# Layer 1's silu from the exponential's table with a VectorE reciprocal, and the last chunk's DMAs begun from two queues

## The chip, the cores and the metric

The kernel runs on one core of one Trainium2 chip. The metric is the device time of one execution in microseconds (us). The kernel before took 1212.17 us (median of three runs, 1210.58 to 1214.08). A core has a matrix engine (PE, which writes only to PSUM), VectorE (DVE), ScalarE (ACT), GpSimd (POOL) and a queue engine (SP); each works through its own list of instructions in order and waits on semaphores for the others. DMAs are begun by an instruction on SP, ACT or POOL.

## The reference

Two transformer layers over x of shape 2 x 1024 x 256, as 16 tiles of 128 rows. Each layer normalises x, and adds an attention and a feed-forward part of the same normalised input:

```python
xn = layernorm(x); x = x + attn0(xn) + ffn0(xn)
xn = layernorm(x); x = x + attn1(xn) + ffn1(xn)
```

The change is in layer 1. Its feed-forward part, with ternary weights `wq_gu` (2048 x 256) and `wq_p` (256 x 1024), is

```python
gate, up = split(xn @ wq_gu.T)          # 1024 columns each
h = silu(gate) * up                     # silu(g) = g / (1 + exp(-g))
out = rms_norm(h) @ wq_p.T
```

Its attention is odd: in every token, the 16 heads of 16 values attend to each other (a 16 x 16 softmax per token), with a rotary embedding before and an output projection `wo` after.

## The kernel before, in words

Layer 0 runs until about 797 us of the profiled execution and is not touched. Layer 1 (`layer1`, L390) treats x in four chunks of 512 tokens, in the order 0, 1, 3, 2. The order of the work is written down ahead of time: `at(delay, f)` puts a piece of work in a heap with a due time, and L673 to L675 take the pieces out in order of due time; PE keeps exactly that order (`manual_schedule` for PE), while the other engines' lists are put in order by a scheduler.

Per chunk there are four *blocks* b of attention and eight *units* hc of the feed-forward part, two units to a block. The pieces, with their lines:

- `project` (L429): the q, k, v projections of 128 tokens. PE writes `pqk` and `pv`; VectorE makes two products with the rotary tables (L442), POOL adds them (L448), ScalarE copies `pv` out (L456). `turn` (L459) transposes on PE (`pt`, L464), ScalarE copies (L465), and SP sends the result through DRAM into the slots (`qkv`, L467 and L469).
- `scores` (L478): PE writes `sq` (L484) to a buffer of four banks that exists once (`ps_s`, bufs=1); VectorE takes the maximum (L492), which goes through DRAM into a row of the slots (L494, L497).
- `turn_v`, `shifted` (L503, L513): PE transposes v (`vt`, L508), then writes the shifted scores `sk` (L519) to the same one `ps_s` buffer, and ScalarE takes the exponential `p` (L527). The next block's `sq` needs the buffer back, and so waits for `p`.
- `weighted`, `normalise`, `turn_back` (L530, L545, L559): `acc` (L534), copied to `o` (L542); transposed to `ot` (L548); VectorE's reciprocal `z` of the 16 sums (L550) and the product `on` (L552); `ob` (L564), copied to `rows` (L565). After the fourth block of a chunk the rows go through DRAM with four DMAs (`orows`, L574) and come back with two (`turned`, L578), then `attended` (L582) multiplies by `wo` (`ao`, L585) and adds to x (L586).
- `ffn_unit` (L598): eight matmuls, four for the gate and four for the up half, into two PSUM banks `ps[0]`, `ps[1]` of the pool `ps_gu`. The pool has two banks in all, so a unit's gate matmuls wait until the last reader of the previous unit's `ps[0]` is done, and its up matmuls until the last reader of `ps[1]` is. ScalarE takes silu of `ps[0]` (L616), VectorE multiplies by `ps[1]` (L617), POOL squares and sums (L621, L623).
- `ffn_scale`, `ffn_out` (L625, L636): the sum over the hidden columns (`pss`, L629), its inverse root (a Sqrt on ScalarE, L145), and the second matmul `f1o` (L640), added to x by VectorE (L648).

`done` (L591) sends a tile of x to the output once both parts are in (L594). All small PE results of the pieces above share the PSUM pool `ps_m` of two banks.

In a middle block PE's order is: `acc`, `pt`, first unit, `ot`, `vt`, second unit, `ob`, `sk`, `pqk`, `pv`, then `sq` of the next block. In the last chunk there is no `project` left, so `sq` follows `sk` directly. In the block that holds the previous chunk's `f1o`, the matmuls of `f1o` stand between the units.

Silu, Exp and Sqrt are in different function tables of ScalarE here: between them stands an `ACT_TABLE_LOAD`.

Of the kernel before, what the change touches and what calls it, by code (L numbers as in the profile page):

```python
# [10 lines left out]
F32 = mybir.dt.float32  # L11
# [3 lines left out]
AF = mybir.ActivationFunctionType  # L15
ALU = mybir.AluOpType
# [3 lines left out]
P = 128  # L20
# [28 lines left out]
def two_layers(ctx: ExitStack, tc: tile.TileContext, a: dict, out: bass.AP):  # L49
    nc = tc.nc  # L50
# [6 lines left out]
    xs = [cp.tile([P, D], F32, tag=f"x{i}", name=f"x{i}") for i in range(NT)]  # L57
# [16 lines left out]
    for name, op, fill, sign in (  # L74
# [5 lines left out]
        for e in range(2):  # L80
            for t in range(2):
                part = m[HALF * e : HALF * e + HALF, t, :]
                nc.gpsimd.affine_select(
                    out=part,
                    in_=part,
# [304 lines left out]
    def layer1(w, wgu, wp, cs, sc):  # L390
# [7 lines left out]
        scale = 1.0 / HD**0.5  # L398
        with ExitStack() as es:
            pool = es.enter_context(tc.tile_pool(name="l1", bufs=2))  # L400
# [6 lines left out]
            chunks = (0, 1, 3, 2)  # L407
# [4 lines left out]
            for n in range(2):  # L412
                q, k, v = (pool.tile([P, NH, P], F32, tag=f"{x}{n}", name=f"{x}s{n}", bufs=1) for x in "qkv")
                nc.gpsimd.memset(v, 1.0)
                for s in range(4):
                    nc.sync.dma_start(
                        out=k[S * s + HD : S * s + HD + 9], in_=a["same"][0, :, None, :].to_broadcast([9, NH, P])
                    )
                    nc.sync.dma_start(
                        out=q[S * s + HD : S * s + HD + 8], in_=a["same"][1, 0:8, None, :].to_broadcast([8, NH, P])  # L420
# [124 lines left out]
            def normalise(c, b, o):  # L545
                ps = ps_m.tile([P, 4, 4, S], F32, tag="m", name=f"ot{c}{b}")
                for r in range(4):
                    nc.tensor.transpose(ps[:, r].rearrange("p s d -> p (s d)"), o[:, r, :], ident)  # L548
                z = pool.tile([P, 4, 4, 1], F32, tag="z1", name=f"z1_{c}{b}")
                nc.vector.reciprocal(z, ps[:, :, :, HD : HD + 1])  # L550
                on = won[b % 2]
                nc.vector.tensor_tensor(  # L552
                    on[:, :, :, 0:HD], ps[:, :, :, 0:HD], z.to_broadcast([P, 4, 4, HD]), ALU.mult
                )
                at(0.9, lambda: turn_back(c, b, on))
# [3 lines left out]
            def turn_back(c, b, on):  # L559
                if b == 0:  # L560
                    rows[c] = pool.tile([P, NH, P], F32, tag="rows", name=f"rows{c}", bufs=1)
                ps = ps_m.tile([P, 4, P], F32, tag="m", name=f"ob{c}{b}")
                for r in range(4):
                    nc.tensor.transpose(ps[:, r], on[:, r].rearrange("p s d -> p (s d)"), ident)  # L564
                nc.scalar.copy(  # L565
                    rows[c].rearrange("p h (t r) -> p (h t) r", r=16)[:, :, 4 * b : 4 * b + 4],
                    ps.rearrange("p r n -> p n r"),
                )
                if b < 3:
                    return  # L570
                scr = dram.tile([D, 4, P], F32, tag="orows", name=f"orows{c}")
                turned = pool.tile([P, 2, 4, P], F32, tag="turned", name=f"turned{c}", bufs=1)
                for s in range(4):
                    nc.sync.dma_start(  # L574
                        out=scr[:, s].rearrange("(h d) t -> d h t", d=HD), in_=rows[c][S * s : S * s + HD]
                    )
                for k in range(2):
                    nc.sync.dma_start(out=turned[:, k], in_=scr[k * P : (k + 1) * P])  # L578
                for s in range(4):
                    at(2.2 + 0.4 * s, lambda s=s: attended(c, s, turned))  # L580

            def attended(c, s, turned):  # L582
                ps = ps_m.tile([P, D], F32, tag="m", name=f"ao{c}{s}")
                for k in range(2):
                    nc.tensor.matmul(ps, turned[:, k, s], wo[:, k, :], start=(k == 0), stop=(k == 1))  # L585
                nc.vector.tensor_add(xs[4 * c + s], xs[4 * c + s], ps)  # L586
                done(4 * c + s)
# [3 lines left out]
            def done(t):  # L591
                parts_done[t] += 1
                if parts_done[t] == 2:
                    nc.sync.dma_start(out=out[t // 8, (t % 8) * P : (t % 8 + 1) * P, :], in_=xs[t])  # L594

            hidden = {}

            def ffn_unit(n, hc):  # L598
                if hc == 0:
                    hidden[n] = [], pool.tile([P, 512], F32, tag="ss", name=f"ss{n}")  # L600
                hs, ss = hidden[n]
                if hc % 2 == 0:
                    hs.append(pool.tile([P, 2, 512], F32, tag="h", name=f"h{n}_{hc}", bufs=6))
                h = hs[-1][:, hc % 2, :]
                nm = f"{n}_{hc}"
                ps = [ps_gu.tile([P, 512], F32, tag="gu", name=f"f1gu{nm}_{g}") for g in range(2)]
                for g in range(2):
                    for k in range(2):
                        nc.tensor.matmul(  # L609
                            ps[g],  # L610
                            wgu[:, k, g * HID + hc * P : g * HID + (hc + 1) * P],
                            xnT[n][:, k, :],
                            start=(k == 0),
                            stop=(k == 1),
                        )
                nc.scalar.activation(h, ps[0], AF.Silu)  # L616
                nc.vector.tensor_mul(h, ps[1], h)  # L617
                sq = ss
                if hc:
                    sq = pool.tile([P, 512], F32, tag="sq", name=f"sq{nm}")  # L620
                nc.gpsimd.tensor_tensor(sq, h, h, ALU.mult)  # L621
                if hc:
                    nc.gpsimd.tensor_tensor(ss, ss, sq, ALU.add)  # L623
# [12 lines left out]
            def ffn_out(n, i, inv):  # L636
                hs = hidden[n][0]
                po = ps_m.tile([P, D], F32, tag="m", name=f"f1o{n}_{i}")
                for hc in range(NHC):
                    nc.tensor.matmul(  # L640
                        po,
                        hs[hc // 2][:, hc % 2, i * P : (i + 1) * P],
                        wp[:, hc, :],
                        start=(hc == 0),
                        stop=(hc == NHC - 1),
                    )
                x_i = xs[4 * n + i]
                nc.vector.scalar_tensor_tensor(x_i, po, inv[:, i : i + 1], x_i, ALU.mult, ALU.add)  # L648
                done(4 * n + i)
# [6 lines left out]
            queue = []  # L656

            def at(delay, f):
                heapq.heappush(queue, (now + delay, next(counter), f))

            counter = itertools.count()
            for p, c in enumerate(chunks):
                for i in range(4):
                    at(8.0 * (p - 1) + 2.0 * i - 0.4 if p else 0.9 * i - 5.0, lambda c=c, i=i: project(c, i))
                for b in range(4):
                    at(8.0 * p + 2.0 * b, lambda c=c, b=b: scores(c, b))
                for hc in range(NHC):
                    at(8.0 * p + hc - 4.7, lambda c=c, hc=hc: ffn_unit(c, hc))
                at(8.0 * p + 8 - 4.7 + 0.6, lambda c=c: ffn_scale(c))
# [3 lines left out]
            while queue:  # L673
                now, _, f = heapq.heappop(queue)
# [583 lines left out]
```

## Time and profile before

| what | value |
|---|---|
| median of three runs | 1212.17 us |
| the profiled execution: its own time | 1211.61 us |
| the profiled execution: span in the trace | 1209.9 us |
| granted PE clock over the span | 0.897 of full speed |
| PE busy | 1026.2 us (85%) |
| VectorE busy | 741.5 us (61%) |
| ScalarE busy | 571.7 us (47%) |
| GpSimd busy | 348.4 us (29%) |
| layer 1 (800 to 1210 us): PE, VectorE, ScalarE, GpSimd busy | 367.1, 117.7, 137.9, 94.1 us |

The columns of a line of the groups are: line, engine, operation, result<-operands with their shapes, count | busy us in all, mean ns of one | idle us of the engine just before them, and what ended it. In the timeline they are start, duration, engine, line, operation, and in brackets the idle time before and its releaser. Matmul ends are modelled: the next matmul's start is a better mark than the end of the one before.

### The profile page before, as it was taken

How to read it: one execution, taken by the hardware profiler on the slowest of the kernel's cores; microseconds unless marked ns; L12 is line 12 of the kernel's file. 1: busy time of each engine (PE TensorE's matmuls, PEld its weight loads, DVE VectorE, ACT ScalarE, POOL GpSimd, SP SyncE). 2: the span in 40 equal slices, each digit the busy share in tenths (PEclk: the TensorE clock that was granted, in tenths of full speed). 3: DMA queues.
4: the chain of work that ended last, by engine and by line, in shares of the span. 5: the costliest groups of instructions: out<-in, count | busy, mean ns of one | idle time of the engine just before them, and what ended most of it. 6: DMA issues, size and time to landing. Idle time of an engine off the chain costs nothing.

```text
span 1209.9 us, 18918 instructions
## 1 busy us (share of the span) xinstructions
PE 1026.2 (85%) x7228; PEld 490.2 (41%) x7228; DVE 741.5 (61%) x1416; ACT 571.7 (47%) x990; POOL 348.4 (29%) x400
## 2 busy tenths in 40 slices
PE   5464888896888989897989998988999999998884
PEld 2232332232232222232323333344676676675673
DVE  6677988995877998789895889162223323322220
ACT  1113353661645757576766776731414414424421
POOL 2023233314144021612125337553313213212100
PEclk8676796996898989898999999998999999998885
DMA  6631001103001010101010110047211421411202
GB/s 194 158 91 37 22 15 38 27 2 90 1 20 33 2 26 18 35 1 24 4 27 2 25 27 5 3 49 114 41 28 46 75 41 45 80 36 29 45 11 53
DMA packets 79011, 48.99 MB, mean 40 GB/s; under 512 B 31720, under 2 KB 73704, under 8 KB 78920
## 3 DMA queue, kind: packets, MB, share of 16 engines
q1 hardware_dynamic: 75960, 43.58, 16.9%
q0 software_dynamic: 2960, 4.20, 1.6%
q8 instruction: 57, 0.93, 0.3%
q14 instruction: 34, 0.28, 0.1%
HBM read 33.59 MB, written 15.73 MB: 41 GB/s over the span
## 4 chain that ended last, share of the span: by engine, by line
PE 55%; DVE 26%; ACT 5%; issue 4%; POOL 4%; DMA 4%; SPq 1%; ACTq 0%; POOLq 0%; DVEq 0%
DVE mx L858 14%; PE f1gu L609 9%; PE acc L940 8%; PE s L910 7%; PE f1o L640 5%; PE m L846 4%; PE sk L519 3%; PE sq L484 3%; PE gu L283 3%; ACT p L527 2%; PE m L823 2%; PE acc L534 1%; PE ao L585 1%; PE pqk L435 1%; ACT p L920 1%
## 5 line engine op out<-in xcount | busy, mean ns | idle before, releaser
L858 DVE TENSOR_REDUCE mx<-m 128x1 f32<-128x512 f32 (+3 forms) x608 | 373.1, 654 | 101.5 <-PE m L846 63.1
L920 ACT ACTIVATE p<-s 128x512 f32<-128x512 f32 x576 | 307.1, 604 | 146.3 <-PE s L910 144.8
L940 PE MATMUL acc<-p,v 128*9 128x512 f32 x1152 | 173.7, 626 | 0.6 <-ACT o L949 0.2
L846 PE MATMUL m<-k,qmain 64*128 64x512 bf16 (+3 forms) x384 | 96.6, 376 | 49.2 <-DVE mx L858 33.0
L924 POOL TENSOR_SCALAR_AFFINE_SELECT p<-p 128x512 f32<-128x512 f32 x128 | 84.6, 685 | 170.1 <-ACT p L920 169.9
L609 PE MATMUL f1gu<-xnT,wgu 128*128 128x512 f32 x256 | 118.5, 607 | 0.0
L846 PE MATMUL m<-kmain,qmain 64*128 64x512 bf16 (+3 forms) x384 | 82.8, 336 | 22.9 <-DVE mx L858 20.7
L846 PEld LDWEIGHTS <-qmain 64*128 64x128 bf16 x768 | 50.4, 101 | 88.4 <-issue 62.9
L621 POOL TENSOR_TENSOR sq<-h 128x512 f32<-128x512 f32 x28 | 29.2, 1041 | 190.1 <-DVE h L617 190.1
L617 DVE TENSOR_TENSOR h<-f1gu,h 128x512 f32<-128x512 f32 x32 | 22.1, 692 | 99.7 <-PE f1gu L609 96.4
L910 PE MATMUL s<-qlast,k 35*128 35x512 bf16 x288 | 66.5, 411 | 14.6 <-DMA qlast<-mscr 14.6
L910 PE MATMUL s<-qmain,k 64*128 64x512 bf16 x288 | 68.6, 412 | 11.8 <-ACT ob L251 6.2
L823 PEld LDWEIGHTS <-ident_h 64*128 64x128 bf16 x832 | 44.9, 97 | 82.5 <-issue 60.3
L823 PE MATMUL m<-mask_q,ident_h 64*128 64x128 bf16 (+3 forms) x832 | 75.3, 222 | 2.5 <-DVE mx L858 2.2
L910 PE MATMUL s<-qmain,kmain 64*128 64x512 bf16 x288 | 64.0, 391 | 6.0 <-ACT p L920 3.2
L910 PEld LDWEIGHTS <-k 64*128 64x128 bf16 (+1 forms) x576 | 21.2, 97 | 115.7 <-issue 108.2
L609 PEld LDWEIGHTS f1gu<-xnT,wgu 128*128 128x128 f32 x256 | 48.0, 197 | 49.2 <-issue 49.1
L492 DVE TENSOR_REDUCE m<-sq 128x16 f32<-128x2048 f32 x16 | 36.7, 2292 | 45.3 <-PE sq L484 43.8
L910 PE MATMUL s<-qlast,klast 35*128 35x512 bf16 x288 | 61.3, 387 | 0.0
L640 PE MATMUL f1o<-k,h 128*128 128x256 f32 x256 | 60.4, 393 | 0.0
L640 PEld LDWEIGHTS f1o<-k,h 128*128 128x128 f32 x256 | 50.1, 197 | 8.7 <-issue 1.1
L983 POOL TENSOR_TENSOR x<-x,aos 128x256 f32<-128x256 f32 x16 | 13.1, 817 | 140.1 <-ACT aos L982 140.0
(265 smaller groups left out, 1572.4 us busy)
## 6 DMA issues: line engine op xcount, KB each, us to landing
qmain<-qscr SPq DMA_DIRECT2D x64, 96.0 KB
qkv<-all SPq DMA_DIRECT2D x16, 384.0 KB
qscr<-ptq SPq DMA_DIRECT2D x32, 96.0 KB
x<-in_x SPq DMA_DIRECT2D x16, 128.0 KB
qmain<-qscr SPq DMA_DIRECT2D x32, 64.0 KB
qs<-qkv SPq DMA_DIRECT2D x16, 128.0 KB
ks<-qkv SPq DMA_DIRECT2D x16, 128.0 KB
vs<-qkv SPq DMA_DIRECT2D x16, 128.0 KB
```

The lines of the kernel that those rows point to most:

```text
L283: nc.tensor.matmul(ps, wg[:, u, k, hc * P : (hc + 1) * P], xq[:, k, :], start=(k == 0), stop=(k == 1))
L484: nc.tensor.matmul(ps[:, s, r, :], columns(q, slice(S * s, S * s + HD + 8), 4 * b + r), columns(k, slice(S * s, S * s + HD + 8), 4 * b + r ...
L492: nc.vector.tensor_reduce(m, ps, AX.X, ALU.max, negate=True)
L609: nc.tensor.matmul(ps[g], wgu[:, k, g * HID + hc * P : g * HID + (hc + 1) * P], xnT[n][:, k, :], start=(k == 0), stop=(k == 1),)
L640: nc.tensor.matmul(po, hs[hc // 2][:, hc % 2, i * P : (i + 1) * P], wp[:, hc, :], start=(hc == 0), stop=(hc == NHC - 1),)
L823: nc.tensor.matmul(out[e][:, :, lo:], ident_h[rows, t, :], rhs.to_broadcast([HALF, out[e].shape[1], P - lo]), start=start and t == 0, stop ...
L846: nc.tensor.matmul(sc[e][:, s * width : (s + 1) * width], qst[b, i][0][rows, p, :], kst[b][0][rows, p // 4, lo : lo + width], start=not fo ...
L858: reduced = nc.vector.tensor_reduce(mx[b, i][:, part, e, pairs[0] : pairs[0] + n], sc[e][:, : n * width].rearrange("p (s k) -> p s k", s=n ...
L910: nc.tensor.matmul(sc[e], kst[b][n][rows, u, j * P : (j + 1) * P], qst[b, i][n][rows, 4 * u : 4 * u + 4, :], start=n == 0, stop=n == 1,)
L920: nc.scalar.activation(p, sc[e], AF.Exp, scale=scale)
L924: nc.gpsimd.affine_select(out=by_head, in_=by_head, compare_op=ALU.is_ge, fill=0.0, base=0, pattern=[[0, 4], [1, P]], channel_multiplier=-1,)
L940: nc.tensor.matmul(acc[32 * s : 32 * s + HD0 + 1, :], vst[b][:, j, 4 * G + s, :], ps[s], start=(j == 0), stop=(j == i),)
```

## The change

In `ffn_unit` silu(gate) is computed as gate times 1 / (1 + exp(-gate)): ScalarE takes the exponential of the gate bank into an SBUF tile `e` (one buffer), and VectorE adds one, takes the reciprocal, and multiplies by the gate bank; then the product with the up bank follows as before. The gate bank has a second reader now, on VectorE. Exp is also what L527 uses.

For the last chunk in the order (chunk 2), half of the `orows` and `turned` DMAs and the outputs of its odd tiles are issued by ScalarE instead of SP.

```diff
@@ turn_back
                 turned = pool.tile([P, 2, 4, P], F32, tag="turned", name=f"turned{c}", bufs=1)
+                queues = (nc.sync, nc.scalar if c == chunks[-1] else nc.sync)
                 for s in range(4):
-                    nc.sync.dma_start(
+                    queues[s % 2].dma_start(
                         out=scr[:, s].rearrange("(h d) t -> d h t", d=HD), in_=rows[c][S * s : S * s + HD]
                     )
                 for k in range(2):
-                    nc.sync.dma_start(out=turned[:, k], in_=scr[k * P : (k + 1) * P])
+                    queues[k].dma_start(out=turned[:, k], in_=scr[k * P : (k + 1) * P])
@@ done
                 if parts_done[t] == 2:
-                    nc.sync.dma_start(out=out[t // 8, (t % 8) * P : (t % 8 + 1) * P, :], in_=xs[t])
+                    queue = nc.scalar if t // 4 == chunks[-1] and t % 2 else nc.sync
+                    queue.dma_start(out=out[t // 8, (t % 8) * P : (t % 8 + 1) * P, :], in_=xs[t])
@@ ffn_unit
-                nc.scalar.activation(h, ps[0], AF.Silu)
+                e = pool.tile([P, 512], F32, tag="e", name=f"e{nm}", bufs=1)
+                nc.scalar.activation(e, ps[0], AF.Exp, scale=-1.0)
+                nc.vector.tensor_scalar(e, e, 1.0, None, ALU.add)
+                nc.vector.reciprocal(e, e)
+                nc.vector.tensor_mul(h, ps[0], e)
                 nc.vector.tensor_mul(h, ps[1], h)
```

In the changed file the exponential is L621, the addition L622, the reciprocal L623, the product with the gate L624 and the product with the up half L625.

## The prediction

> **What bounds the kernel now.** I read the page's slices first, for where the engines are full:
>
> ```profile
> PE   5464888896888989897989998988999999998884
> DVE  6677988995877998789895889162223323322220
> ```
>
> Layer 1 is the last third. There PE is full and VectorE has two thirds free, so PE's list sets the time, and what counts is where PE waits. The timeline of one middle block shows the unit that changes:
>
> ```profile
> 1004.06 3.60 PE L609 MATMUL f1gu<-xnT,wgu 128*128 128x512 f32 x8
> ...
> 1004.87 1.28 ACT L616 ACT_TABLE_LOAD   x1
> ...
> 1007.77 0.69 DVE L617 TENSOR_TENSOR h<-f1gu,h 128x512 f32<-128x512 f32 x1 [2.79 <-PE f1gu L609]
> ...
> 1008.38 3.60 PE L609 MATMUL f1gu<-xnT,wgu 128*128 128x512 f32 x8
> 1010.37 0.60 ACT L616 ACTIVATE h<-f1gu 128x512 f32<-128x512 f32 x1 [1.19 <-PE f1gu L609]
> ...
> 1014.98 1.28 ACT L527 ACT_TABLE_LOAD   x1 [1.93 <-PE sk L519]
> 1016.27 1.88 ACT L527 ACTIVATE p<-sk 128x2048 f32<-128x2048 f32 x1
> ...
> 1018.20 2.17 PE L484 MATMUL sq<-ks,qs 24*128 24x128 f32 x32 [0.50 <-ACT p L527]
> ```
>
> See three things. The block's two units start 4.32 us apart (1004.06, 1008.38) on the same two banks, and the second does not wait. The gate bank can be read 1.99 us after a unit's start (1010.37 - 1008.38). And `sq` waits 0.50 for the exponential `p`, ahead of which stands a table load. The waits give the sum of the last:
>
> ```profile
> PE sq L484 <- ACT p L527: 13.7, 10, 3.3
> ```
>
> Seven of the ten waits are 0.50 to 0.60, three are 3.33 (the last chunk, nothing between `sk` and `sq`). For prices, the groups of VectorE by form:
>
> ```profile
> L617 DVE TENSOR_TENSOR h<-f1gu,h 128x512 f32<-128x512 f32 x32 | 22.1, 692 | 99.7 <-PE f1gu L609 96.4 <-PE ob L564 3.4
> L959 DVE RECIPROCAL z<-ot 128x16 f32<-128x16 f32 x32 | 8.0, 249 | 30.2 <-PE ot L955 30.2
> L193 DVE TENSOR_SCALAR few<-few 128x1024 f32<-128x1024 f32 x6 | 4.3, 721 | 0.0
> L146 DVE RECIPROCAL rs_yf<-rs_sf 128x4 f32<-128x4 f32 x4 | 0.7, 175 | 1.8 <-ACT rs_sf L145 1.8
> ```
>
> A reciprocal grows by 74 ns from 4 to 16 elements a partition, 6.2 ns an element. The last view is PE's clock, in half-microsecond windows after an idle time of 2.07 us that ended at 822.27 (columns: window, its length, PE busy, granted clock, DMA share, GB/s):
>
> ```profile
> 822.50:823.00 0.50, 0.50 (x2) 1.00 0.27 82
> 823.00:823.50 0.50, 0.50 (x2) 0.89 0.86 246
> 823.50:824.00 0.50, 0.50 (x2) 0.50 1.23 159
> ```
>
> The clock is halved, and stays so until 826.8.
>
> **The change: ScalarE.** The changed program's list has 18 table loads where there were 43: 25 x 1.28 = 32 us less on ScalarE. Exp on the gate bank is priced as Silu was, 0.60. On PE's path only the waits of `sq` shrink: seven by 0.53 (they vanish, since 1.28 is more) and two of the three long ones by 1.28 (1107 and 1126 us; at 1169.76 a Sqrt stands before, so that load remains): 3.7 + 2.6 = **-6.3**. The loads ahead of Silu were covered already (1004.87 to 1006.16, gate ready at 1006.05).
>
> **The reciprocal.** No 128x512 one is in the trace. From the 128x16 row with 6.2 ns an element: 0.249 + 496 x 0.0062 = 3.3; with the steeper other 128x4 row (171 ns, 6.5 to 6.7 ns) 3.5. I take r = 3.4. Below, the end is 0.69, the price of L617, an ordinary operation on this shape; above, 4.4, if the growth from 4 to 8 elements (29 ns, 7.2 ns each) is the truer slope, with 15% for the unknown.
>
> The skill's page "VectorE: DVE Perf Modes", section "First, the fixed hardware budget", says that the reciprocal is an iterative divide with a repeat count of 8. If that means 8 cycles an element at the 0.96 GHz that the skill gives, an estimate is 4.3 plus overhead; the sum would then be that of the second rival. The trace's 6.2 ns would be 6 such cycles; I go by the row.
>
> **A middle block, step by step,** from the first unit's start: gate bank readable 1.99; Exp to 2.59; hop 0.06; the addition, half of L193's 0.72 plus a little, 0.38, to 3.03; reciprocal from 3.06 to 6.46. VectorE's new order puts `z` (0.25) next, to 6.74; then the product with the gate (0.69 as L617), to 7.46; hop 0.06. PE may start the second unit at 7.52 instead of 4.32: **3.2** of stall. Queued behind the reciprocal are also `on` (to 7.9) and the up product (8.6); `ob` and the second unit's up matmuls come later than that. The second unit's own chain ends some 16 after the first start; then the two rotary products, POOL's sum and `pt`, just before the next unit at 20.4 - tight, but VectorE carries only about 15 us in it. Pairs of this kind: 860.98, 913.86, 931.27, 950.27, 1004.06, 1021.80, 1039.83, 1093.62 and 1111.33: 9 x 3.2 = **+28.8**.
>
> **The first chunk** (800 to 850 us). VectorE is full there. Unit 0's reciprocal goes ahead of the rotary products, so unit 1 (809.68) starts 2.6 late; its addition comes only when the layernorm's `xn` are done (817.7), so unit 2 is 6.7 late. The 2.07 of wait before `pqk` at 822.27 (a DMA) absorbs part: 4.5 late. `pt` at 827.77 waits for rotary products behind unit 2's reciprocal: 5.5. Units 3 and 4 (828.27) are back to back, 3.44 apart: 3.8 more. The 1.55 of DMA wait at 838.6 vanishes: about 7.2 late; units 5 and 6 add 1.2. Together **+8.5**.
>
> **The rest.** Where `f1o` stands between the units nothing waits for a bank, but `z`/`on` come behind the reciprocal, and `ot`'s bank is returned later: 1.3 + 0.6 + 0.6 = **+2.5** for the blocks at 885, 974 and 1063. The last unit (1130.14) has no second; its `ob` was at 5.47, now behind `on` at 8.0: **+2.5**.
>
> **POOL.** A VectorE operation on SBUF can be held while POOL works: the 128x4 product of L147 at 807.76 took 1.02 instead of 0.16 and ended when POOL's L621 did (807.73 to 808.77). The second unit's addition meets POOL's sums so: 0.9 late, within the slack, but `pt` becomes tight. 0 to 0.5 a block; I take **+1**.
>
> **PE's clock.** Of six idle times of 1.5 to 3.4 us in layer 1 at full clock (804, 820, 838, 1104, 1123, 1166 us), five were followed by clock 0.50. A unit caught in it took 4.77 (1111.33) or 5.67 (843.11) instead of 3.60: 1.2 to 2.1 more. Ten new stalls have some 3.0 of idle each: 10 x 5/6 x 1.2 = 10, less 2 for the two 3.33 waits that become 2.05: **+8**. Ends: -2 (never) and +18.
>
> The skill's "TensorE: Matmul & The Clock Gate", section "What's actually happening", has the clock halved after at least one idle window of about 3.4 us. By it, 3.0 of idle would not do so, and the sum would be 8 lower; but here 2.07 did.
>
> **The tail.** Four `orows` issues take SP 3.23, but the DMA engines then work at a share of 0.66 to 0.92 (sum of the six 1-us windows from 1191: 4.3), so two queues can end them at most 0.9 sooner; the second `turned` 0.4 sooner; the last output is issued when x is ready, no gain. ScalarE issues no DMA in this trace; POOL's issues took 0.54 to 0.79 where SP's outputs took 0.34, so up to 0.4 lost. Nothing is queued behind on ScalarE. **-0.5**, ends -1.3 and +0.5.
>
> **The sum:** 28.8 + 8.5 + 2.5 + 2.5 + 1 + 8 - 6.3 - 0.5 = +44.5 on the profiled 1211.6 = 1256.1; the median lies 0.56 above that execution: **1257**.
>
> **The rivals.**
> *The reciprocal is as cheap as any operation on this shape (not slower).* Then r = 0.69; the pair's stall is only what `z`'s wait for `ot` leaves, 0.8 x 9 = 7, the first chunk's delays go into its DMA waits, and the saved 6.8 pay for it: 1212 to 1213. It decides from r = 0.7 downward; each microsecond of r above costs about 13. Against it: the slope of three sizes. For it: all are tiny.
> *VectorE and POOL become the bound.* r = 4.4: the pair's stall is 4.2, and `pt` then waits for rotary products queued behind the second unit's products and POOL's sums, 1.1 more: 9 x 2.1 + 4 = 23 more, 1280. For it: the 7.2 ns slope; POOL's holding. Against: VectorE's 15 us in a block of 20.
> *The stalls are milder:* the clock does not fall and the first chunk's delay goes into its DMA waits: 44.5 - 8 - 8 - 2 = +26, 1239.
>
> **How the numbers follow.** Likeliest case 0.68 (1244 to 1270: clock and start at their ends), VectorE/POOL bound 0.13, milder 0.13, cheap reciprocal 0.06. Range 1234 to 1280: it leaves out the cheap case and the far end of the second rival. About 0.3% (3.6 us) is what a measurement can tell from no change. The cheap case splits into faster 0.03 and same 0.03; everything else is slower, 0.94.
>
> **What would show it.** L623 with a mean of about 3.4 us x32; PE's f1gu, idle 0.0 before, waiting for VectorE's L624 about ten times 3 us; half clock after many of these stalls; `sq` waiting for `p` only in the last chunk; 18 table loads. Wrong if L623 is near 0.7 us, if PE waits at `pt` for POOL, or if the gaps leave the clock at 1.00.

## The result, and the profile after

The changed kernel takes 1262.56 us (median of four runs, 1261.91 to 1263.13), where the kernel before took 1213.09 beside it (1210.58 to 1214.08). The ratio is 1.0417, with a 95% interval of 1.0402 to 1.0433: slower by 4.2%, and 5.6 us above the forecast. The profiled execution is one of 1261.91, with a span of 1260.1 (before 1209.9, so +50.2) at a mean granted clock of 0.889.

The page's slices, after (VectorE's last third was 223323322220):

```profile
PE   5455888888889898979899989868899898897884
DVE  6677988987858987898958892667556556646520
```

VectorE is not full in layer 1, and yet its work sets the time: PE's row has gaps (an 8 or a 6 where there were 9s). The page's groups name the two instructions, and show what the reciprocal costs:

```profile
L612 PE MATMUL f1gu<-xnT,wgu 128*128 128x512 f32 x256 | 135.8, 680 | 34.0 <-DVE h L624 34.0
L623 DVE RECIPROCAL e<-e 128x512 f32<-128x512 f32 x32 | 107.3, 3353 | 1.1
L622 DVE TENSOR_SCALAR e<-e 128x512 f32<-128x512 f32 x32 | 14.4, 449 | 77.4 <-ACT e L621 77.4
```

A reciprocal takes 3.353 us. The unit's matmuls wait 34.0 us for the gate's product L624, where they waited for nothing before, and they are also busy for 17.3 us longer (135.8 against 118.5). PE's waits from 796 us on (total, times, longest):

```profile
PE f1gu L612 <- DVE h L624: 34.0, 13, 3.5
PE ao L587 <- DMA turned<-orows: 11.2, 1, 11.2
PE pt L464 <- POOL qk L448: 8.0, 4, 5.1
PE sq L484 <- ACT p L527: 7.4, 3, 3.3
PE ob L564 <- DVE on L552: 4.4, 3, 3.1
```

Before, these were 0.0, 10.4, 3.3, 13.7 and 0.9. Two waits of before are gone (`pqk` for `all`, 2.1, and `sq` for the DMA of `ks`, 1.6). All of PE's idle time grew by 36.8 us and its busy time by 13.4 (1026.2 to 1039.6); the two make the 50.2. The busy part is work at a lower clock: the instructions are the same, and the unit's matmuls alone are 17.3 longer. Other matmuls that had met the halved clock before are shorter in return (the first `f1o` took 4.69 at 879.42, and takes 3.72 at 899.07).

One middle block shows how both come about (timeline: start, duration, engine, ..., in brackets the idle time before):

```profile
932.60 3.60 PE L612 MATMUL f1gu<-xnT,wgu 128*128 128x512 f32 x8
...
934.52 0.60 ACT L621 ACTIVATE e<-f1gu 128x512 f32<-128x512 f32 x1 [1.13 <-PE f1gu L612]
935.15 0.43 DVE L622 TENSOR_SCALAR e<-e 128x512 f32<-128x512 f32 x1 [1.62 <-ACT e L621]
935.61 3.35 DVE L623 RECIPROCAL e<-e 128x512 f32<-128x512 f32 x1
...
938.88 0.19 DVE L550 RECIPROCAL z<-ot 128x16 f32<-128x16 f32 x1
939.00 0.69 DVE L624 TENSOR_TENSOR h<-f1gu,e 128x512 f32<-128x512 f32 x1
...
939.75 5.40 PE L612 MATMUL f1gu<-xnT,wgu 128*128 128x512 f32 x8 [2.66 <-DVE h L624]
```

The second unit starts 7.15 us after the first instead of 4.32, because its bank is read last by L624. And it then takes 5.40 us instead of 3.60. PE's clock in the same unit (window, length, PE busy, granted clock, DMA share, GB/s) says why:

```profile
939.50:940.00 0.50, 0.25 (x1) 1.00 0.13 4
940.50:941.00 0.50, 0.50 (x2) 0.95 0.76 225
941.00:941.50 0.50, 0.50 (x2) 0.50 1.03 188
943.50:944.00 0.50, 0.50 (x2) 0.50 0.00 0
944.50:945.00 0.50, 0.50 (x3) 1.00 0.00 0
```

The gap of 2.66 ends at 939.75; 1.2 us later the clock falls to half, and it stays there for some 3.4 us. So a gap like this is paid twice. Not every gap is: the unit at 1163.52 waits 2.66 too and takes 3.70 (the last section compares such gaps).

### The profile page after: what moved, and what is told of

The parts are those of the page before. It is cut to its first block, busy times and chain, and to the rows that moved or that the text cites. A ratio compares the mean times of both kernels' runs of the same rounds, so it can differ in the third digit from the quotient of the medians.

```text
span 1260.1 us, 18967 instructions
## 1 busy us (share of the span) xinstructions
PE 1039.6 (82%) x7228; PEld 491.5 (39%) x7228; DVE 879.7 (70%) x1512; ACT 540.3 (43%) x965; POOL 347.6 (28%) x400
## 4 chain that ended last, share of the span: by engine, by line
PE 49%; DVE 33%; DMA 4%; POOL 4%; ACT 4%; issue 4%; SPq 1%; ACTq 0%; POOLq 0%; DVEq 0%
DVE mx L866 13%; PE f1gu L612 8%; PE acc L948 8%; PE s L918 7%; DVE e L623 5%; PE f1o L648 5%; PE m L854 3%; PE gu L283 3%; PE sk L519 2%; PE sq L484 2%; PE ao L587 1%; PE m L831 1%; PE pqk L435 1%; PE acc L534 1%; DMA qmain<-qscr 1%
## 5 line engine op out<-in xcount | busy, mean ns | idle before, releaser
L948 PE MATMUL acc<-p,v 128*9 128x512 f32 x1152 | 177.0, 635 | 0.6 <-ACT o L957 0.2
L612 PE MATMUL f1gu<-xnT,wgu 128*128 128x512 f32 x256 | 135.8, 680 | 34.0 <-DVE h L624 34.0
L623 DVE RECIPROCAL e<-e 128x512 f32<-128x512 f32 x32 | 107.3, 3353 | 1.1
L612 PEld LDWEIGHTS f1gu<-xnT,wgu 128*128 128x128 f32 x256 | 53.7, 220 | 95.3 <-issue 57.5
L622 DVE TENSOR_SCALAR e<-e 128x512 f32<-128x512 f32 x32 | 14.4, 449 | 77.4 <-ACT e L621 77.4
L621 ACT ACTIVATE e<-f1gu 128x512 f32<-128x512 f32 x32 | 19.1, 597 | 114.3 <-PE f1gu L612 114.2
L918 PEld LDWEIGHTS <-k 64*128 64x128 bf16 (+1 forms) x576 | 21.3, 97 | 117.6 <-issue 109.6
```

The source lines that it names most:

```text
L612: nc.tensor.matmul(ps[g], wgu[:, k, g * HID + hc * P : g * HID + (hc + 1) * P], xnT[n][:, k, :], start=(k == 0), stop=(k == 1),)
L623: nc.vector.reciprocal(e, e)
L918: nc.tensor.matmul(sc[e], kst[b][n][rows, u, j * P : (j + 1) * P], qst[b, i][n][rows, 4 * u : 4 * u + 4, :], start=n == 0, stop=n == 1,)
L948: nc.tensor.matmul(acc[32 * s : 32 * s + HD0 + 1, :], vst[b][:, j, 4 * G + s, :], ps[s], start=(j == 0), stop=(j == i),)
```

## The experiments

Two theories stand against each other, A and B where the expectations name them so. A is the prediction's: the gate bank is held by VectorE's chain, PE waits for it, and PE's clock falls after the wait. B is the main rival, that VectorE's list, in order and with the reciprocal in it, is what PE waits for, whichever bank is held; the expectations price it as the work of VectorE and POOL. The parts of the change and the terms of the sum are then taken one by one.

**The silu alone.** Only `ffn_unit` is changed; all DMAs stay on SP.

```diff
-                nc.scalar.activation(h, ps[0], AF.Silu)
+                e = pool.tile([P, 512], F32, tag="e", name=f"e{nm}", bufs=1)
+                nc.scalar.activation(e, ps[0], AF.Exp, scale=-1.0)
+                nc.vector.tensor_scalar(e, e, 1.0, None, ALU.add)
+                nc.vector.reciprocal(e, e)
+                nc.vector.tensor_mul(h, ps[0], e)
```

> The silu part alone, with the last chunk's DMAs and outputs begun by SP as before. From the two traces, the way from the end of the last copy of rows to the end took 19.62 us before and 19.58 after, so the queue part should be worth nothing: 1262 to 1263, the same as the whole change. By the prediction's step for the tail (-0.5, ends -1.3 and +0.5) it would be 1263, at most 1264. If the two queues cost something (the turned rows landed 0.8 us later after the change), it would be 1261 to 1262.

Measured: 1262.77 us, ratio 1.0424 (1.0404 to 1.0444). PE's waits for the bank, `pt`, `sq` and `ob` are those of the whole change to the tenth (34.0, 8.0, 7.4, 4.4). All of the cost is in this part.

**The queues alone.** Only the DMAs of the last chunk are changed; the silu stays as it was.

```diff
-                    nc.sync.dma_start(
+                    queues[s % 2].dma_start(
...
-                    nc.sync.dma_start(out=turned[:, k], in_=scr[k * P : (k + 1) * P])
+                    queues[k].dma_start(out=turned[:, k], in_=scr[k * P : (k + 1) * P])
...
+                    queue = nc.scalar if t // 4 == chunks[-1] and t % 2 else nc.sync
```

> The queue part alone, silu by its own table as before. Worth nothing: 1212.5 to 1213.5. By the prediction's step 1212.6, ends 1211.8 and 1213.6. If two queues are really better in the tail, 1211 or less.

Measured: 1214.35 against 1212.38, ratio 1.0019 (1.0006 to 1.0032): no gain, and a loss at the edge of what can be measured, just above the range expected. The wait of `ao` for `turned` is 11.2 instead of 10.4. Why it grew is tried further down.

**The reciprocal's price.** The changed kernel with an ordinary product in the reciprocal's place, so that silu is not computed; all else, the order of dependencies included, is kept.

```diff
-                nc.vector.reciprocal(e, e)
+                nc.vector.tensor_mul(e, e, e)
```

> Leaves out the reciprocal: a product e*e of the same shape stands in its place (so silu is not computed, only the same number of operations). Theory A, the gate bank is held too long: the release comes at about 1.99 + 0.60 + 0.06 + 0.43 + 0.69, then z's wait for ot, then 0.69, some 5.1 after a unit's start against 4.32, so a stall of 0.8 or less and no fall of the clock: 1211 to 1217, PE's wait for L624 under 10 us in all instead of 34. Theory B, VectorE's and POOL's work is the limit: VectorE has 85 of the 138 added us taken off, so about 62% of the 49.5 us come back: 1230 to 1236.

Measured: 1205.78, ratio 0.9959 (0.9942 to 0.9975): 56.8 us below the changed kernel, even below A's 1211 to 1217 and far from B's 1230 to 1236. The groups of this run, by form:

```profile
L612 PE MATMUL f1gu<-xnT,wgu 128*128 128x512 f32 x256 | 116.6, 598 | 1.3 <-DVE h L624 1.3
L623 DVE TENSOR_TENSOR e<-e 128x512 f32<-128x512 f32 x32 | 22.2, 692 | 1.1
```

So three passes over the gate on VectorE cost nothing by themselves; the 2.66 us that one instruction is longer cost it all, with what follows from them. The timeline shows VectorE's order here:

```profile
1003.26 3.60 PE L612 MATMUL f1gu<-xnT,wgu 128*128 128x512 f32 x8
...
1006.99 0.69 DVE L624 TENSOR_TENSOR h<-f1gu,e 128x512 f32<-128x512 f32 x1
1007.60 0.25 DVE L550 RECIPROCAL z<-ot 128x16 f32<-128x16 f32 x1
...
1007.74 3.70 PE L612 MATMUL f1gu<-xnT,wgu 128*128 128x512 f32 x8
```

The gate's product stands ahead of `z`, so a second unit is late by 0.16 (4.48 against 4.32), where the prediction, with `z` first, had 0.8 left.

**Giving the banks back before the reciprocal.** ScalarE copies the gate out, the up product comes first, and addition, reciprocal and last product follow on SBUF alone. The result is the same; ScalarE has one more copy a unit (0.58).

```diff
                 nc.scalar.activation(e, ps[0], AF.Exp, scale=-1.0)
-                nc.vector.tensor_scalar(e, e, 1.0, None, ALU.add)
-                nc.vector.reciprocal(e, e)
-                nc.vector.tensor_mul(h, ps[0], e)
-                nc.vector.tensor_mul(h, ps[1], h)
+                nc.scalar.copy(h, ps[0])
+                up = nc.vector.tensor_mul(h, ps[1], h)
+                with tc.issue_after(up.ins):
+                    nc.vector.tensor_scalar(e, e, 1.0, None, ALU.add)
+                    nc.vector.reciprocal(e, e)
+                    nc.vector.tensor_mul(h, h, e)
```

> The reciprocal stays and VectorE's work is the same (add, reciprocal, two products), but both PSUM banks are released early: ScalarE also copies the gate bank to SBUF, VectorE multiplies that by the up bank first, and only then come the addition, the reciprocal and the last product, all in SBUF. Theory A (bank held): the gate bank is free 3.3 us and the up bank about 4.3 us after a unit's start, when the next needs them at 4.32 and 6.04: no stall, no fall of the clock, and the 6.3 us of shorter waits of sq are kept; left is the first chunk, where VectorE is full (8 to 13 us): 1213 to 1221. Theory B (work): 1255 to 1265, since VectorE and POOL have the same to do.

Measured: 1252.04, ratio 1.0343 (1.0322 to 1.0363), a little under B's range and far above A's. Only 10.5 of some 50 us come back, so A alone does not hold: without the bank's hold the kernel is nearly as slow. The waits of PE show where the time went. For the bank it is 0.0 now, but

```profile
PE pt L464 <- POOL qk L448: 20.6, 11, 5.8
...
PE ob L564 <- DVE on L552: 11.0, 12, 4.1
```

were 8.0 and 4.4 in the changed kernel. The timeline of a middle block gives the way from the reciprocal to `pt`:

```profile
938.45 3.35 DVE L626 RECIPROCAL e<-e 128x512 f32<-128x512 f32 x1
...
943.05 0.68 DVE L442 TENSOR_TENSOR qk<-pqk,r_sc 128x512 f32<-128x512 f32 x1
...
943.73 1.26 POOL L633 TENSOR_TENSOR ss<-ss,sq 128x512 f32<-128x512 f32 x1
...
944.95 1.26 POOL L448 TENSOR_TENSOR qk<-qk,qk 128x512 f32<-128x512 f32 x1
946.26 0.66 PE L464 MATMUL pt<-ident,qk 128*128 128x128 f32 x4 [2.61 <-POOL qk L448]
946.76 5.29 PE L612 MATMUL f1gu<-xnT,wgu 128*128 128x512 f32 x8
```

The second unit's reciprocal stands on VectorE ahead of the rotary products; POOL has that unit's own sum (L633) to finish before it adds them, and `pt` is late by 2.61; the next unit meets the halved clock (5.29). It is the order of VectorE's list that holds PE here, not the amount of its work: from 870 to 1165 us VectorE is busy for 178.1 of 295 us. This is the mechanism of B, but not its size for the changed kernel: there the bank's wait holds PE back first, and `pt` comes just in time (0 to 0.15 in most middle blocks). The two waits are in a row behind the same instruction, and the second shows when the first is taken away. In the first chunk the edit does less than its name says: there ScalarE's next exponential waits four times, 19.3 us in all, for the one buffer `e` (L621 <- DVE L627), and the copy of the gate is queued behind it. How much of the 1252 is due to that was not tried; a second buffer of `e` would show it.

**The clock by itself.** In the changed kernel, in ten blocks, the four transposes of v (`vt`, L508) are done six times over into the same bank, so that PE works through the time in which it would wait. The result is the same.

```diff
-                for r in range(4):
-                    nc.tensor.transpose(pv[:, r, :], columns(v, slice(0, P), 4 * b + r), ident)
+                for _ in range(6 if b != 2 and (c != 2 or b == 0) else 1):
+                    for r in range(4):
+                        nc.tensor.transpose(pv[:, r, :], columns(v, slice(0, P), 4 * b + r), ident)
```

> The whole change, and in the ten blocks where PE waits for the gate bank the four transposes of vt are done six times over (same result): some 2.2 us of PE work in a gap of 2.66 us of idle time, so nothing on the path gets longer by itself. If the second units take 5.1 to 5.4 us instead of 3.6 because the idle gap lets the clock fall, the fillers keep it up and some 9 x 1.6 = 14 us come back: 1247 to 1252. If they are slow for another reason (PSUM or the engines beside it), nothing comes back: 1262 to 1264. If transposes do not count as work for the clock: the same 1262 to 1264, with a granted clock of 0.50 in the second units still.

Measured: 1250.98, ratio 1.0331 (1.031 to 1.0352): 11.6 us faster than the changed kernel, by work that nobody needs. The timeline of a middle block:

```profile
929.18 3.60 PE L613 MATMUL f1gu<-xnT,wgu 128*128 128x512 f32 x8
...
933.05 2.88 PE L509 MATMUL vt<-ident,vs 128*128 128x128 f32 x24
936.32 3.70 PE L613 MATMUL f1gu<-xnT,wgu 128*128 128x512 f32 x8 [0.39 <-DVE h L625]
```

The second unit starts no sooner (7.14 after the first), but runs 3.70 and not 5.40. So 11.6 of the loss are the clock's; the wait itself is still there, as busy time.

**The first chunk.** The changed kernel, with the old Silu in the first chunk (n == 0) alone.

```diff
+                if n == 0:
+                    nc.scalar.activation(h, ps[0], AF.Silu)
+                else:
...
```

> The whole change, but the first chunk's eight units keep silu's table. In the trace the first scores' sk came 13.8 us later, counted from the first unit, with the change; the prediction had 8.5 for this part and its share of the clock's fall. If that delay is the first chunk's own (VectorE full until 817 us, rotary products behind the reciprocals) it comes back: 1248 to 1252. If it is only moved and taken up later by other waits, 1255 to 1262.

Measured: 1241.25, ratio 1.0245 (1.0223 to 1.0268): 21.3 us less, more than was expected. Relative to the first unit's start, the first `sk` comes at 50.25 instead of 65.66, which is 15.4; and the pair formed by the chunk's last unit and the next chunk's first runs without a wait (its starts are 4.33 apart instead of 7.14, and its second unit takes 3.60 instead of 5.09), worth 2.8 + 1.5 = 4.3 more. In the two profiled executions layer 1, from its first unit to the end, takes 437.7 instead of 458.0 us; of these 20.3 the two are 19.7. The delay is the first chunk's own and is not made up later.

**Another table.** Silu by Tanh, from the kernel before: silu(g) = g (1 + tanh(g/2)) / 2. The factor 1/2 is left in h, and the rms norm takes it out, with its epsilon multiplied by 4. Same result, one VectorE pass more than before.

```diff
-                nc.scalar.activation(h, ps[0], AF.Silu)
+                nc.scalar.activation(h, ps[0], AF.Tanh, scale=0.5)
+                nc.vector.scalar_tensor_tensor(h, h, 1.0, ps[0], ALU.add, ALU.mult)
...
-                inv = rsqrt(pool, ms, 4, RMS_EPS, f"f1_{n}")
+                inv = rsqrt(pool, ms, 4, 4.0 * RMS_EPS, f"f1_{n}")
```

> The kernel before, with silu(g) as g (1 + tanh(g/2)) / 2: Tanh shares a table with Exp in layer 0 (no table load stands between them there), VectorE does one operation of about 0.7 us on the gate bank, and the half is left out and the constant under the root made four times as large, which gives the same output. It keeps the shorter waits of sq (-6.3) and has no reciprocal: the gate bank is free about 3.4 us after a unit's start, before 4.32. Expected 1204 to 1208. If one more VectorE operation in the chain already stalls PE (pt, ob), 1210 or more.

Measured: 1203.62, ratio 0.9942 (0.9924 to 0.9959): 0.6% faster than the kernel before, a little under the 1204 to 1208 expected. By its groups,

```profile
L617 DVE SCALAR_TENSOR_TENSOR h<-h,f1gu 128x512 f32<-128x512 f32 x32 | 22.0, 687 | 65.9 <-ACT h L616 65.9
L616 ACT ACT_TABLE_LOAD x4 | 5.1, 1283 | 0.1
```

Tanh and Exp change without a load here (4 loads at L616 where there were 15), and the gate bank is held for one pass of 0.69. PE's wait for the bank is 0.0, and `sq` waits 7.4 for `p` as in the changed kernel. This is what the change could have given.

**Tanh with the two queues.** The edit of the queues on top of that.

> The tanh form with the last chunk's DMAs begun from two queues as in the change. In every trace so far the wait of the last output projection for turned is 10.35 to 10.43 us with SP alone and 11.1 to 11.4 with two queues. If that 0.8 us is real and is all, this is 0.8 us slower than the tanh form on SP alone: 1204 to 1205 against 1203 to 1204, about 0.9945 to 0.996 of the kernel before. If the queues cost 2 us or more, as the timed ratio of the queue part alone (1.0019) has it, 1205.5 or more.

Measured: 1203.95, ratio 0.9935 (0.991 to 0.996), and `turned` waits 11.1. Against Tanh with SP alone no difference in time can be told.

**Half of the queue edit.** The kernel before, with the four `orows` begun from two queues, and `turned` and the outputs from SP.

```diff
-                    nc.sync.dma_start(
+                    queues[s % 2].dma_start(
                         out=scr[:, s].rearrange("(h d) t -> d h t", d=HD), in_=rows[c][S * s : S * s + HD]
```

> The kernel before, with only the four orows DMAs of the last chunk from two queues; turned and the outputs by SP. If the 0.8 us comes from the two turned DMAs running at once from two queues, the last projection's wait is back at 10.4 us or a little under, and the time is that of the kernel before (ratio 0.999 to 1.001). If orows is the slow one, the wait stays at 11.1 to 11.4.

Measured: 1212.94 against 1211.91, ratio 1.0004 (0.9987 to 1.0022). The tail of this run, and then that of the changed kernel, by the timelines:

```profile
1198.42 0.81 SPq L580 DMA_DIRECT2D turned<-orows  x2
...
1201.19 6.55 PE L587 MATMUL ao<-wo,turned 128*128 128x256 f32 x16 [10.32 <-DMA turned<-orows]
```

```profile
1240.54 0.82 SPq L576 DMA_DIRECT2D orows<-rows  x2
1240.55 0.87 ACTq L576 DMA_DIRECT2D orows<-rows  x2
...
1247.36 0.36 ACTq L580 DMA_DIRECT2D turned<-orows  x1
1247.42 0.34 SPq L580 DMA_DIRECT2D turned<-orows  x1
...
1251.05 5.63 PE L587 MATMUL ao<-wo,turned 128*128 128x256 f32 x16 [11.16 <-DMA turned<-orows]
```

From the first `orows` issue to the first `turned` issue it is 6.90 us in the one and 6.82 in the other, and `ao` waits 10.3 here as it waited 10.4 in the kernel before. From there to `ao` it is 2.77 with both `turned` on SP (1198.42 to 1201.19) and 3.69 with one on each queue (1247.36 to 1251.05). So the growth of the wait by 0.8 to 0.9 comes with the pair of `turned` begun at once; halving the issue time of `orows` bought nothing. The landings in the traces show how. The first matmul of `ao` needs only the first half of `turned`. With both halves on SP that half has landed 2.63 us after the first issue, and the other at 3.29; with one on each queue the two land at 3.39 and 3.56, and the half that is needed first is the later one.

At the end of the program less of it is left. From the first `turned` issue to the end it is 0.4 to 0.5 more with two queues in each of three pairs of runs (13.11 against 12.71 for the queues alone and the kernel before, 12.75 against 12.26 for the whole change and the silu alone, 12.73 against 12.22 with Tanh). The 0.19% of the queues alone are 2.3 us. In the profiled executions layer 1 takes 410.0 from its first unit to the end, against 409.2 before, and the rest of their difference lies ahead of layer 1 (its first unit starts at 803.63 instead of 800.72), where nothing was changed.

## Why the prediction was right, and where its sizes were wrong

The sign and the mechanism held: PE waits for the gate bank behind the reciprocal, and for the most part pays again at half clock. That the forecast missed by only 5.6 us is in part luck: the clock came out 5.4 above its term, and the middle pairs 3.3 below theirs. By its own steps:

*The reciprocal:* 3.4 was taken, 3.353 measured. The slope from 4 to 16 elements a partition carried to 512. The Trainium skill's "VectorE: DVE Perf Modes", section "First, the fixed hardware budget", gives a repeat count of 8 for it; read as 8 cycles an element this would be 4.3, and the measurement decides against that reading: 3.353 over 512 is 6.5 ns.

*The middle pair:* 3.2 of delay predicted, 2.83 measured (7.15 - 4.32), 9 x 2.83 = 25.5 where the sum had 28.8. Of each 2.83 PE is idle for 2.66. The predicted end of `z` was too late: it took 0.19 instead of 0.25, and the gate's product began 3.39 after the reciprocal's start where the sum had 3.68.

*The first chunk:* +8.5 predicted; the first `sk` is 13.8 later after the first unit's start (65.66 against 51.88). Of this 5.0 are three units at half clock (835.75, 844.29 and 862.44: 4.99, 5.40 and 5.38 instead of 3.60), which the prediction counted with the clock. The other 8.8 are its 8.5. (The halved clock had met this stretch before too, 843.11: 5.67. So PE's busy time in it is 2.8 longer and its idle time 11.0.) `pt` at 834.85, after the largest wait of 5.1, is 5.7 late counted from the first unit, where 5.5 had been predicted.

*PE's clock:* +8 predicted, 13.4 measured. This is the term that was mis-sized most. The unit's matmuls alone grew by 17.3, all of PE's work by 13.4, and filling the gaps bought back 11.6. The sum took ten gaps, five of six followed by the fall, at 1.2 each; in the trace 11 units were caught, most at 1.5 to 1.8 (5.1 to 5.4 instead of 3.60), and one at 3.2 (1040.56: 6.76). The smaller of the two rows that it had (4.77 and 5.67) was taken for the price, and most came out between the two. Its rule, that an idle time of 1.5 us or more mostly brings the fall, left out that the trace of before has falls with no wait above 0.6 us ahead of them (878.00, 942.85, 1144.24). The Trainium skill's "TensorE: Matmul & The Clock Gate", section "What's actually happening", has the clock fall after at least one idle window of about 3.4 us, and calls that window free-running, at 3413 ns. The trace agrees with such a window (the last section), but not with a wholly idle one: 1.20 us of work in the 3.41 before 940.95 did not prevent the fall, and gaps of 2.66 were enough.

*Where `f1o` stands between:* +2.5 predicted, 2.1 measured as three waits of `f1o` and `ao` (0.7 each). *The last unit's `ob`:* +2.5 predicted, 2.6 measured: it starts 8.05 after its unit (1183.71 - 1175.66) instead of 5.47, a wait of 3.1 where there was one of 0.7. *`pt` and POOL:* +1 predicted, next to nothing in the middle blocks.

*The waits of `sq`:* -6.3 predicted, -6.3 measured (13.7 to 7.4).

*The tail:* -0.5 predicted, with +0.5 as its upper end; the wait of `ao` grew by 0.8, and counted from the first `turned` issue the end came 0.5 later than with the silu alone. The step that failed is "the second `turned` 0.4 sooner": it was issued 0.3 sooner after the first and landed no sooner (10.21 us after the first `orows` issue, 10.26 before), while the half that `ao` needs first landed 0.8 later (10.38, where it was 9.61).

With the measured sizes, in PE's times: of the 50.2, 13.4 are busy time and 36.8 idle time. The idle part is 23.9 for the nine pairs (9 x 2.66; the rest of the 2.83 counts as busy), 11.0 in the first chunk (17.9 against 7.0), 2.1 where `f1o` stands, 2.4 at the last `ob` and 0.8 at `turned`, less 6.3 at `sq`; and 1.6 lie ahead of layer 1's first unit (802.09 against 800.72), in work that the change does not touch. Of the 36.8 idle, 1.3 are left, 0.9 of them in the wait of `sk` for the DMA of `qs` (1.1 where it was 0.2).

*The rivals.* That the reciprocal be cheap was tested by the product in its place: its condition would have given 1205.8, a gain, and not 1212 to 1213. Its price went wrong with the 0.8 that `z` was to leave. From there to the real reciprocal it is 56.8 us over 2.66, 21 per microsecond of r and not 13, since the clock's part came on top; on a straight line between the two points, which no run in between supports, no change would lie at r = 1.0 and not 0.7. The bound by VectorE and POOL did not come at r = 3.35, but the wait that it names, `pt` for POOL, lies close behind: freeing the banks brought it out, by the order of VectorE's list. The milder case fell with the clock.

## What to carry to other kernels

Price an operation by the buffer it keeps and by what is queued behind it, not by its engine's free time: 3.35 us a unit on an engine that was two thirds idle cost about 50 us, first through the PSUM bank that they held and, behind that, through their place ahead of products that PE needs, and a third as much again as PE's idle time was lost to PE's clock (13.4 after 36.8). Before mending such a wait, look for the next one behind the same instruction; moving it off the bank gave back a fifth, and removing it (a function from the same table as its neighbour, with the constant folded into the norm) gave it all and more. Do not count a DMA as sooner because it is issued sooner; look at when the part lands that the next step needs first.

## What the hardware showed that was not expected

- PE's clock changed only on a fixed grid here. In layer 1 of the trace of before the falls (823.39, 840.45, 878.00, 942.85, 1106.69, 1123.76, 1144.24, 1168.13) are whole multiples of 3.413 us apart, and each half-clock stretch is one or more such steps long. Where a gap lies on the grid goes with whether it is paid. In the changed kernel, by steps of the grid (window, length, PE busy, granted clock, DMA share, GB/s):

```profile
818.07:821.48 3.41, 2.00 (x11) 1.00 0.80 128
821.48:824.90 3.42, 1.93 (x5) 1.00 0.57 165
937.54:940.95 3.41, 1.20 (x3) 1.00 0.27 56
940.95:944.36 3.41, 3.41 (x5) 0.50 0.28 42
```

Of the wait of 2.66 before 939.75, 2.2 lie in one step, which is left with 1.20 us of work, and the next step is at half clock. The longer wait of 2.90 before 822.97 is divided between two steps of some 2 us of work each, and the unit after it took 3.70. PE's busy time is not the whole rule: the step before the fall at 942.85 was full (3.41 of 3.41 busy, most of it `sk`). What else counts, no run here shows; nor did one move a gap along the grid.

- Transposes repeated in the gaps kept the clock at 1.00 there (936 to 938), and so were worth 11.6 us.
- Two reads of the same size begun at the same time from SP and ScalarE let PE begin 3.69 us after the issue, against 2.77 when SP began both one after the other: side by side they landed at 3.39 and 3.56, one after the other at 2.63 and 3.29, and PE needs the first half first.
- VectorE's addition on SBUF took 0.43 in most units; with the repeated transposes it took 0.97 from 938.97, where POOL's sum ran from 938.39 to 939.66 beside it, and its mean there was 597 ns against 449.
- Tanh needs no table load next to Exp here, where Silu did: 5 loads at the two lines L616 and L527 where there were 30.
